# Fetching more tiles of embedding rows on SyncE and ScalarE, with a smaller descriptor store

## The chip, the core and the metric

The kernel runs on one core of a Trainium2 chip. The core has five engines that run side by side, each with a queue of instructions worked off in order: TensorE (PE; its weight loads are shown as PEld), VectorE (DVE), ScalarE (ACT), GpSimd (POOL) and SyncE (SP). Sixteen DMA engines move data between the chip's main memory and the core's on-chip memory; a transfer is issued by SP, ACT or POOL and tells of its landing by a semaphore. The metric is the device time of one execution in microseconds (us); lower is better.

## What is computed

A recommender's ranking network. For 16384 users there are 69 items each (`batch_user`) and one label item. Every item is a row of 96 floats in a table of 100001 rows. Each row is weighted by a small attention network against the label's row, the weighted rows are summed into 10 groups, and three layers follow.

```python
u  = emb[batch_user]                      # 16384 x 69 x 96
ql = emb[batch_label[:, 0]]               # 16384 x 96
q  = broadcast(ql)
z  = concatenate([q, u, q - u, q * u])    # 384 wide
h  = dice(z @ W1 + b1, a1)                # 64 wide
att = (h @ W2 + b2) @ W3 + b3
pre = where(batch_user < ITEM_NUM, u * att, 0)
pooled = einsum('gf,bfe->bge', window, pre)
x  = concatenate([pooled, ql])
h  = dice(bn(x @ Wf1 + bf1), af1)
h  = dice(bn(h @ Wf2 + bf2), af2)
out = h @ Wf3 + bf3
```

`dice` is a sigmoid gate, `bn` a constant scale. All is float32.

## The kernel before

The users are cut into 32 blocks of 512. A block's 512 x 69 rows are 69 chunks (64 of the main fields, 5 of the tail's), a chunk is four tiles of 128 rows, one row to a partition. Two chunks are a pair, and a pair is one step: there are 1104 steps (`NPAIR`). The order on every engine's queue is written out by hand: `plan` holds for each step the pieces of work in their order, and `at(step, ...)` appends to it.

What a step i does, in this order on each queue: every fourth step the attention rows of four pairs (`attend_rows`, PE matmul prow, ACT copy at L416) and a step later `spread` (PE patt, DVE rw); `hidden(i - 2)`: PE matmuls into ph (L399, L403), ACT's two activations (L405, L406), DVE's product y (L407); `scalar_rows(i)`: ACT's issues; `pool(i - 7)`: PE's acc matmuls on the pair's rows (L325), DVE's copy to pooled (L470); and `fetch(i)`: the rows of pair i are gathered, transposed by PE into two banks ptr (L325), and DVE makes uT (L376) and quT (L379) from each. Between these lie, once in a block, the label rows (`head_gather`, four gathers), and the top layers in ten pieces (`top_steps`, L502, L483, L484). The last eight steps have an order of their own (`CLOSE`).

The rows come in three ways:

- By POOL. `gather` (L266) issues one indirect DMA for a tile of 128 rows: 128 row numbers in, 128 x 96 floats out, into one of the eight places of a buffer u. `upool` has 14 such buffers; a pair's buffer is read by its transposes in step i and by `pool` seven steps later.
- By SP. A tile listed in `SP_CHUNKS` is fetched with 128 single DMAs of one row (384 bytes) each (L301) into a ring of `SP_RING` buffers. The row's address is in a register; `load` (L286) brings a group of addresses from the tile `offsets` into registers.
- By ACT, from `ACT_CHUNKS`, in the same manner, but a few rows in each step (`scalar_rows`), between its activations, into `ACT_RING` buffers.

In a listed chunk it is the fourth tile (`SLOT` = 3) that comes through the ring. PE waits for its semaphore (`wait_for_single`) and reads the ring's buffer in place of u. The first row of a tile into a buffer waits, through the framework, for the buffer's last readers, which are PE's acc matmuls. SP also loads the indices, `ids`, for four blocks at a time (L151), 50 steps ahead of the first of them, in the same queue.

Of the kernel before, what the change touches and what calls it, by code (L numbers as in the profile page):

```python
# [18 lines left out]
P = 128  # L19
# [29 lines left out]

ROW_BYTES = 4 * E  # L50
SLOT = 3
SP_CHUNKS = [2 * (10 * s + 8) + 1 for s in range(109)]
SP_RING = 4
ACT_CHUNKS = [2 * (8 * s + 11) for s in range(136)]
ACT_RING = 3
ACT_ROWS = 16
ACT_STEPS = -(-P // ACT_ROWS)
SINGLES = SP_CHUNKS + ACT_CHUNKS
NSB = (len(SINGLES) + P - 1) // P
NSEM = 8  # L60


def chunk_of(c):
# [52 lines left out]
def rec_kernel(  # L116
# [12 lines left out]
    nc = tc.nc  # L129
# [1 line left out]

    const = ctx.enter_context(tc.tile_pool(name="const", bufs=1))
    ipool = ctx.enter_context(tc.tile_pool(name="ipool", bufs=2))
    upool = ctx.enter_context(tc.tile_pool(name="upool", bufs=14))
    tpool = ctx.enter_context(tc.tile_pool(name="tpool", bufs=4))
    ypool = ctx.enter_context(tc.tile_pool(name="ypool", bufs=6))
    rpool = ctx.enter_context(tc.tile_pool(name="rpool", bufs=2))
# [137 lines left out]
    class Singles:  # L275

        def __init__(self, name, engine, kind, chunks, first, buffers, group):
            self.name, self.engine, self.kind, self.group = name, engine, kind, group
            self.chunks, self.first, self.buffers = chunks, first, buffers
            self.sems = [tc.alloc_semaphore(f"{name}{k}") for k in range(NSEM)]  # L280
            self.given = [0] * NSEM

# [12 lines left out]
        def fetch(self, s, start, stop):  # L295

            b, k = self.buffers[s % len(self.buffers)], s % NSEM
            for r in range(start, stop):
# [295 lines left out]
    def at(step, *work):  # L594
        plan.setdefault(step, []).extend(work)

    by_sync = Singles("sp", nc.sync, mybir.EngineType.SP, SP_CHUNKS, 0, range(SP_RING), 32)
    for s, m in enumerate(SP_CHUNKS):
        at(max(0, m // 2 - 6), lambda s=s: by_sync.fetch(s, 0, P))

    by_scalar = Singles(
        "act",
        nc.scalar,
        mybir.EngineType.Activation,
        ACT_CHUNKS,
        len(SP_CHUNKS),
        range(SP_RING, SP_RING + ACT_RING),
        2 * ACT_ROWS,
    )
    turn = {}  # L610
    for s, m in enumerate(ACT_CHUNKS):
        for k in range(ACT_STEPS):
            turn.setdefault(m // 2 - 2 - ACT_STEPS + k, []).append((s, k * ACT_ROWS, min(P, (k + 1) * ACT_ROWS)))

    def scalar_rows(i):

        for s, start, stop in turn.get(i, []):
            by_scalar.fetch(s, start, stop)

    c = NPAIR - CLOSE  # L620
    for i in range(c):
        if i >= 3 and (i - 3) % 4 == 3:
            at(i, rows_of(i - 6, 4))
        if i >= 3:
            at(i, tails_of(i - 3))
        if i >= 4 and (i - 4) % 4 == 3:
            at(i, spread_of(i - 7, 4))
        if i >= 2:
            at(i, hidden_of(i - 2))
        at(i, lambda i=i: scalar_rows(i))  # L630
        if i < c - CLOSE:
            if i >= POOL_LAG:
                at(i, pool_of(i - POOL_LAG))
        else:

            for k in {0: (-15, -14), 1: (-13,), 3: (-12, -11), 4: (-10, -9), 7: (-8, -7)}.get(i - c + 8, ()):
                at(i, pool_of(c + k))
        at(i, fetch_of(i))
# [116 lines left out]
```

## Time and profile before

| what | value |
|---|---|
| time, median of 3 executions | 10925.68 us (10925.35 to 10929.42) |
| profiled execution's own time | 10926.71 us |
| its span, from the first to the last instruction | 10924.9 us |
| granted TensorE clock, mean | 0.745 |
| POOL gathers | 8587 of u, 128 of q |
| rows issued by SP | 13952 |
| rows issued by ACT | 17408 |
| loads of row addresses | 436 on SP (median 2174 ns), 544 on ACT (median 2182 ns) |

The profile gives each engine's busy time; issues of DMAs, register moves and waits on the queues do not count as busy, so SP has no busy time at all and ACT's is without its row issues. Groups of instructions are named by line and by what they write and read: `u<-in_rows,ids` is a gather of rows. A line such as "2620.1 <-issue 2428.2" gives the idle time of the engine ahead of these instructions, and what ended most of it; "issue" means that nothing in the profile was waited for. In the timeline a name with a q (SPq, ACTq) stands for the engine's queue, and equal instructions are merged with their number behind an x.

### The profile page before, as it was taken

What the parts mean: (1) busy time and instruction counts of PE and PEld (TensorE: products, weight loads), DVE (VectorE), ACT (ScalarE), POOL (GpSimd) and SP (SyncE); (2) the same over time, 40 slices, a digit from 0 to 9 for tenths busy, and PEclk for the clock granted to TensorE, in tenths of its full rate; (3) what the DMA queues carried; (4) which work ended last, traced back from release to release, by engine and by line L of the source; (5) the groups of instructions that cost most, each with busy time, mean ns of one, the idle gap of its engine ahead of it and who ended that gap; (6) DMA issues with size and microseconds to landing.
All of it is one profiled execution on the core that took longest, in us unless ns stands there. A gap on an engine that the chain in (4) does not pass through costs nothing.

```text
span 10924.9 us, 172203 instructions
## 1 busy us (share of the span) xinstructions
PE 8862.0 (81%) x41797; PEld 4319.5 (40%) x41797; DVE 4285.5 (39%) x7535; ACT 1897.5 (17%) x2761; POOL 8226.3 (75%) x8721
## 2 busy tenths in 40 slices
PE   7878878788887888888878778878888887888878
PEld 3333434343333344333433333334343333433335
DVE  4334333333333333433333333333333333333334
ACT  1111111111111111111111111111111111111112
POOL 7777777777777777777777777777777777777776
PEclk7767777777777777767777777777777777777777
DMA  2212211121111212212111121112212112122111
GB/s 49 42 42 44 42 42 41 42 44 42 42 42 42 44 41 42 42 41 44 42 42 41 42 44 42 42 42 42 44 42 42 42 41 44 42 42 41 42 41 36
DMA packets 344467, 458.51 MB, mean 42 GB/s; under 512 B 202354, under 2 KB 202866, under 8 KB 343330
## 3 DMA queue, kind: packets, MB, share of 16 engines
q0 software_dynamic: 278880, 428.92, 18.7%
q1 hardware_dynamic: 29762, 11.82, 0.5%
q10 hardware_dynamic: 34816, 6.75, 0.4%
q8 instruction: 336, 5.51, 0.2%
q14 instruction: 673, 5.51, 0.2%
HBM read 446.74 MB, written 0.07 MB: 41 GB/s over the span
## 4 chain that ended last, share of the span: by engine, by line
POOL 49%; issue 21%; PE 17%; DMA 12%; DVE 0%; ACT 0%; ACTq 0%; POOLq 0%; DVEq 0%
POOL u L266 48%; DMA u<-in_rows,ids 12%; PE p L502 4%; PE acc L325 4%; PE ph L399 3%; PE ph L403 2%; PE ptr L325 2%; POOL q L266 1%; PE prow L414 1%; PE pa L423 1%; PE ph L396 0%; PE ph L401 0%; PE pc L348 0%; PE patt L431 0%; ACTq L301 0%
## 5 line engine op out<-in xcount | busy, mean ns | idle before, releaser
L266 POOL DMA_INDIRECT u<-in_rows,ids x8587 | 8104.3, 944 | 2620.1 <-issue 2428.2
L325 PE MATMUL ptr<-ident,u 128*96 128x128 f32 x8587 | 2002.8, 332 | 1940.1 <-DMA u<-in_rows,ids 1892.9
L407 DVE TENSOR_TENSOR y<-ph,y 128x512 f32<-128x512 f32 x1104 | 763.5, 692 | 4377.1 <-ACT y L406 4119.6
L325 PEld LDWEIGHTS ptr<-ident,u 128*96 128x96 f32 x8587 | 1139.7, 149 | 2701.4 <-DMA u<-in_rows,ids 2262.6
L325 PEld LDWEIGHTS acc<-rw,u 128*96 128x96 f32 x15930 | 1677.0, 187 | 1204.3 <-issue 977.6
L376 DVE COPY uT<-ptr 96x512 f32<-96x512 f32 x2208 | 1494.1, 677 | 1488.6 <-PE ptr L325 1485.2
L325 PE MATMUL acc<-rw,u 128*96 128x20 f32 x15930 | 1792.5, 258 | 57.8 <-DVE rw L436 41.7
L405 ACT ACTIVATE y<-ph 128x512 f32<-128x512 f32 x1104 | 658.6, 597 | 6308.6 <-PE ph L403 5822.7
L399 PE MATMUL ph<-uT,A 128*64 128x512 f32 x4096 | 1649.8, 883 | 0.0
L403 PE MATMUL ph<-quT,wn 96*64 96x512 f32 x4416 | 1585.2, 788 | 0.0
L379 DVE TENSOR_TENSOR quT<-ptr,qT 96x512 f32<-96x512 f32 x2048 | 1380.2, 674 | 0.0
L406 ACT ACTIVATE y<-y,wn,na1c 128x512 f32<-128x512 f32 x1104 | 898.1, 813 | 36.6
L403 PEld LDWEIGHTS ph<-quT,wn 96*64 96x64 f32 x4416 | 440.7, 188 | 1041.5 <-issue 1040.8
L502 PE MATMUL p<-pooled,wf 96*100 96x512 f32 (+1 forms) x1400 | 693.1, 644 | 0.0
L399 PEld LDWEIGHTS ph<-uT,A 128*64 128x64 f32 x4096 | 264.1, 175 | 616.2 <-issue 608.8
L416 ACT COPY row<-prow 128x512 f32<-128x512 f32 (+1 forms) x277 | 161.6, 583 | 1791.9 <-PE prow L414 1179.1
L470 DVE COPY pooled<-acc 96x160 f32<-96x160 f32 x1008 | 419.9, 417 | 117.6 <-PE acc L325 116.9
L414 PE MATMUL prow<-y,v 128*32 128x512 f32 x2208 | 453.6, 891 | 1.4 <-DVE y L407 1.1
L502 PE MATMUL p<-pre,V 96*100 96x512 f32 (+1 forms) x700 | 394.9, 710 | 3.0 <-DVE x L485 2.7
L502 PEld LDWEIGHTS p<-pooled,wf 96*100 96x100 f32 x1400 | 259.5, 198 | 332.6 <-issue 332.6
L436 DVE SCALAR_TENSOR_TENSOR rw<-patt,bb,wn 128x320 f32<-128x320 f32 x554 | 276.2, 539 | 143.6 <-PE patt L431 142.9
L431 PE MATMUL patt<-ident,row 128*128 128x128 f32 x1108 | 224.9, 340 | 25.1 <-DVE pre L424 22.7
(72 smaller groups left out, 2445.8 us busy)
## 6 DMA issues: line engine op xcount, KB each, us to landing
ring<-in_rows ACTq DMA_DIRECT2D x17408, 0.4 KB
ring<-in_rows SPq DMA_DIRECT2D x13952, 0.4 KB
u<-in_rows,ids POOLq DMA_INDIRECT x8587
ids<-in_idx SPq DMA_DIRECT2D x8, 560.0 KB, 3.9
q<-in_emb,ids POOLq DMA_INDIRECT x128
wf<-in_far SPq DMA_DIRECT2D x1, 1209.0 KB, 6.4
wn<-in_near SPq DMA_DIRECT2D x1, 236.0 KB, 2.8
ids<-in_idx SPq DMA_DIRECT2D x1, 140.0 KB, 2.3
```

The costliest lines, as they stand in the source:

```text
L266: nc.gpsimd.indirect_dma_start(out=dst, out_offset=None, in_=table, in_offset=bass.IndirectOffsetOnAxis(ap=index, axis=0),)
L325: ins = op(out, ring[:, at[0]].bitcast(F32) if at else u[:, 4 * (c % 2) + t, :], other, **how)
L376: nc.vector.tensor_copy(uT[j][0:E], ptr)
L379: nc.vector.tensor_tensor(quT[:, j, :].rearrange("e (s f) -> e s f", f=FM), ptr.rearrange("e (s f) -> e s f", f=FM), by_field(q[:, k * NS ...
L399: nc.tensor.matmul(p, As[n % 2][:, k // 4, :], uT[j], start=True, stop=False)
L403: nc.tensor.matmul(p, Wp, quT[:, j, :], start=False, stop=True)
L405: nc.scalar.activation(y, ph, AF.Sigmoid, scale=S_DICE)
L406: nc.scalar.activation(y, y, AF.Identity, bias=a1c, scale=na1c)
L407: nc.vector.tensor_mul(y, ph, y)
L414: nc.tensor.matmul(pr[32 * k : 32 * (k + 1), :], v2, ys[b + k], start=True, stop=True)
L470: nc.vector.tensor_copy(pooled[n][:, :, k * NS : (k + 2) * NS].rearrange("e g s -> e s g"), pa.rearrange("e j s g -> e (j s) g"),)
L502: nc.tensor.matmul(p1, w[:, h * DH : (h + 1) * DH], x, start=(k == 0), stop=(k == KTOP - 1))
```

## The change

- SP's list grows from 109 tiles, one in ten steps, to 199, one in five and a half. Its ring has 8 buffers for 4.
- ACT's list grows from 136 tiles to 170. Its rows are now one stream over all tiles, 20 in each step from step 0 on, where it was 16 in each of the eight steps of a tile. Addresses are still loaded 32 at a time; a step may now end one tile and begin the next. Its ring has 4 buffers for 3.
- A tile of ACT's is used two or three steps after the step that issues its last row; before it was three.
- `upool` has 15 buffers for 14.
- The kernel sets the size of the store that holds POOL's descriptors, in bytes of each partition, to 4096, where it left the framework's own.
- `offsets` grows to 384 columns for 256, as `NSB` follows the number of listed tiles.

```diff
-SP_CHUNKS = [2 * (10 * s + 8) + 1 for s in range(109)]
-SP_RING = 4
-ACT_CHUNKS = [2 * (8 * s + 11) for s in range(136)]
-ACT_RING = 3
-ACT_ROWS = 16
-ACT_STEPS = -(-P // ACT_ROWS)
+SP_CHUNKS = [2 * (int(5.5 * s) + 6) + 1 for s in range(199)]
+SP_RING = 8
+ACT_ROWS = 20
+ACT_CHUNKS = [2 * ((s + 1) * P // ACT_ROWS + 2) for s in range(170)]
+ACT_RING = 4
...
+RING_BYTES = 4096
...
-    upool = ctx.enter_context(tc.tile_pool(name="upool", bufs=14))
+    upool = ctx.enter_context(tc.tile_pool(name="upool", bufs=15))
...
-        2 * ACT_ROWS,
+        32,
     )
-    turn = {}
-    for s, m in enumerate(ACT_CHUNKS):
-        for k in range(ACT_STEPS):
-            turn.setdefault(m // 2 - 2 - ACT_STEPS + k, []).append((s, k * ACT_ROWS, min(P, (k + 1) * ACT_ROWS)))
-
     def scalar_rows(i):
 
-        for s, start, stop in turn.get(i, []):
-            by_scalar.fetch(s, start, stop)
+        row, stop = i * ACT_ROWS, min((i + 1) * ACT_ROWS, len(ACT_CHUNKS) * P)
+        while row < stop:
+            s, start = divmod(row, P)
+            n = min(P - start, stop - row)
+            by_scalar.fetch(s, start, start + n)
+            row += n
...
-    nc = bacc.Bacc("TRN2", target_bir_lowering=False, num_devices=1)
+    nc = bacc.Bacc("TRN2", target_bir_lowering=False, num_devices=1, dynamic_dma_scratch_size=RING_BYTES)
```

## The prediction

> **What bounds the kernel now.** I read the page's head, its groups and its chain first, then POOL's waits, then the chain at the end, and last the queues of SP and ACT, since the change loads these two.
>
> ```profile
> span 10924.9 us, 172203 instructions
> ...
> PE 8862.0 (81%) x41797; PEld 4319.5 (40%) x41797; DVE 4285.5 (39%) x7535; ACT 1897.5 (17%) x2761; POOL 8226.3 (75%) x8721
> ...
> POOL 49%; issue 21%; PE 17%; DMA 12%; DVE 0%; ACT 0%; ACTq 0%; POOLq 0%; DVEq 0%
> ...
> L266 POOL DMA_INDIRECT u<-in_rows,ids x8587 | 8104.3, 944 | 2620.1 <-issue 2428.2
> L325 PE MATMUL ptr<-ident,u 128*96 128x128 f32 x8587 | 2002.8, 332 | 1940.1 <-DMA u<-in_rows,ids 1892.9
> ```
>
> ```profile
> POOL u L266 <- issue: 2428.2, 7958, 0.3
> POOL u L266 <- DMA u<-in_rows,ids: 111.1, 364, 0.3
> ```
>
> POOL's 75% is a full engine: each gather is busy 0.944 us, then 0.30 us pass, and no idle stretch in its waits is longer than 0.3, whoever is named. The first of its 8715 gathers (8587 of u, 128 of q) starts at 3.30 us and the last at 10886.76: 1.2490 us apart on average, 1.2487 after the first hundred. PE waits 1893 us for their rows.
>
> ```profile
> 10748.20 2.47 DMA u<-in_rows,ids
> 10750.67 0.04 issue
> 10750.71 0.45 PE ptr L325
> 10751.16 5.12 PE p L502 x24
> ```
>
> This is the chain near the end. Up to 10748 us (about step 1085) it keeps coming back to a gather; from 10751 it is PE's closing work of some 174 us. So a gather removed before step 1085 takes its 1.2487 us off the end; a later one need not.
>
> **The gathers removed.** Single tiles go from 109+136 = 245 to 199+170 = 369, so POOL issues 124 gathers fewer: 8591. By step 1085 (m//2 counted over the lists) it is 366 against 243, thus 123: 123 x 1.2487 = 153.6 us. A step (one pair of chunks) shrinks from 8715 x 1.249 / 1104 = 9.86 us to 8591 x 1.249 / 1104 = 9.72 us. Every queue that now works more must fit into that.
>
> **SyncE: 25,472 rows instead of 13,952.** The trace has SP with its ring empty at the start, running without a wait:
>
> ```profile
> 6.33 243.65 SPq L301 DMA_DIRECT2D ring<-in_rows  x611
> ...
> SPq L301 <- PE ptr L325: 3556.9, 71, 95.2
> SPq L301 <- PE acc L325: 1324.8, 26, 96.8
> ```
>
> 243.65/611 = 0.399 us a row with the loads of row addresses (TENSOR_LOAD, median 2.17 us, four a tile) among them: 51.0 us a tile. By the tiles one by one, 48.7 us from first to last row and 2.6 to the next tile's first: 51.3 us. The change asks for a tile per 5.5 x 9.72 = 53.5 us, so SP is 96% full, and its 4882 us of waiting on PE nearly vanish. ScalarE's issues beside it do not slow it: rows follow each other at 0.3257 us while ACT issues, 0.3252 while it doesn't. 199 x 51.3 = 10,209 us against some 10,690 up to step 1095, where the last tile is used. With eight buffers a tile's buffer returns after 44 steps, of which it is held for 7 after its use, so the wait for PE at the head of each tile is over by then. Behind that wait in SP's queue stand the ids loads (L151, eight of them); they are placed 50 steps ahead of the block and needed 14 ahead, POOL's lead of 8 steps included 22: 28 steps of cover. The first one now stands behind tile 0, 55 us, and POOL wants it near step 12, 120 us. Cost: 0.
>
> **ScalarE: 21,760 rows, 20 a step for 16.** From two steps without idle time in its queue:
>
> ```profile
> 7013.77 0.60 ACT L405 ACTIVATE y<-ph 128x512 f32<-128x512 f32 x1 [1.31 <-PE ph L403]
> 7014.40 0.81 ACT L406 ACTIVATE y<-y,wn,na1c 128x512 f32<-128x512 f32 x1
> 7014.47 4.87 ACTq L301 DMA_DIRECT2D ring<-in_rows  x16
> 7019.38 0.60 ACT L405 ACTIVATE y<-ph 128x512 f32<-128x512 f32 x1 [4.17 <-PE ph L403]
> 7020.01 0.81 ACT L406 ACTIVATE y<-y,wn,na1c 128x512 f32<-128x512 f32 x1
> 7022.29 5.00 ACTq L301 DMA_DIRECT2D ring<-in_rows  x16
> ```
>
> L405 to the first row is 0.70 us; L406 runs beside the rows; an address load puts 2.21 us in (7022.29-7020.01 against 7014.47-7014.40). Sixteen rows take 4.8 to 5.55 us in this neighbourhood, so twenty 6.0 to 6.9, say 6.3. Loads are now one per 32 rows, 0.625 a step: 1.4. The copy of row (0.58 every fourth step), the top's g pairs and A's copies add 0.15 + 0.14 + 0.03. Sum 8.7 us, ends 8.4 and 9.3, of 9.72: 90% full, still under. What it delays: the next step's L405/L406 stand behind these rows, DVE's y L407 behind those, and behind it uT and quT of the newest pair, which free PE's two ptr banks. PE then starts a step later than it could; but PE has 9.72 - 8862/1104 = 1.7 us of slack a step, and POOL only feels PE after 15 u buffers less the 7 steps of lag: 8 steps, 78 us. In the trace the longest a gather's rows lay before PE took them was 25 us. Cover gone, it costs what ACT exceeds 9.72 by, per step. I take 0.
>
> At the closing PE is the chain. In steps 1073 to 1085 it catches up from 24 us behind POOL; POOL now makes four single tiles there for three, 1.2 to 2.5 us faster. I charge 1 us, ends 0 and 3. The 124 further ring tiles on PE add waits on semaphores: the present 245 ring transposes had no idle time before them. 0.
>
> **The smaller descriptor store and the fifteenth u buffer.** No gather waits for a buffer now, so the fifteenth brings nothing. The store is not seen as a thing in the trace. Lower bound 0: from the hundredth gather to the last the spacing never leaves 1.24 to 1.28 us. Upper bounds: the slow gathers at the start, in bunches such as
>
> ```profile
> 124.14 1.07 POOL L266 DMA_INDIRECT u<-in_rows,ids  x1 [0.30 <-issue]
> 125.51 1.07 POOL L266 DMA_INDIRECT u<-in_rows,ids  x1 [0.31 <-issue]
> 126.89 1.07 POOL L266 DMA_INDIRECT u<-in_rows,ids  x1 [0.30 <-issue]
> ```
>
> which make the first 98 average 1.275 us (128.26-3.30 over 98), 0.0264 more than the rest; and, further off, a gather that has to wait until an earlier one lands (2.47 us from start to landing, 1.5 more than the busy 0.94). Only two gathers are under way at once by that row (2.47/1.249), so I take 0 for any store that holds a handful.
>
> The Trainium skill, DMA: Bandwidth & Descriptors, states under Terms that a descriptor is 16 bytes and under The descriptor swizzle that a full transfer gives each engine nine, one of them the completion; a 4096-byte ring would by that hold 28 gathers, an estimate. No run here shows it.
>
> The same page, under Rules for kernel authors, speaks against the change: small transfers should be coalesced, since under 64 KB one pays mostly overhead, and under Anatomy of one DMA it puts a fixed 2.0 us on each. The rows above show 384-byte transfers leaving one queue every 0.33 us, so the fixed part overlaps. By the rule taken serially a tile would be 128 x 2.0 = 256 us and 199 of them 51 ms; by the row 10.2 ms.
>
> **The sum.** 10924.9 - 153.6 + 1 = 10772.3 us of span; the profiled run's time was 1.8 above its span and the median 1.0 below that run (10926.71 against 10925.68), so 10,773 us.
>
> **Rivals.**
> - *The store makes gathers dearer, and it ends slower than before.* Place: POOL's period. If the start's 0.0264 us stays for all 8591 gathers, +227 us: 11,000 us. It decides from 153/8591 = 0.018 us a gather, or one wait of 1.5 us per 85 gathers. For it: POOL has no idle time to hide anything. Against: after the first hundred nothing recurs, and the start also has the large loads beside it.
> - *SP becomes the bound.* It decides above 53.5 us a tile, 4% over what was measured. With rows at 0.35 us (tails of the spacing reach 0.355) a tile is 124 x 0.35 + 4 x 2.6 = 53.8, and 199 x 53.8 + 4, then some 90 us from step 1095 to the end: 10,800 us; at 54.1, 10,860. For it: never asked to run through before; against: the opening 611 rows did.
> - *The ACT-DVE-PE chain becomes the bound.* At ACT's upper 9.3 us with one L405 (0.60) waited for in every step, a step is 9.9 us; 1104 of them and the 40 us that the span has outside 1104 x 9.86 give 10,970 us; it decides from 9.72 and is slower than before from 9.86. For it: ACT, PE and SP at 90, 83 and 96%. Against: the 78 us of lead, and ACT's rows leave PE two steps.
> - *No change:* the shorter gather stream is given back by PE all through, 10,926. Against: 1893 us of PE's waiting are for gathers, ten times the gain.
>
> **How the numbers follow.** Forecast 0.73; SP 0.11; ACT chain 0.05, of which 0.01 ends faster, 0.02 within 0.2% and 0.02 slower; no change 0.01; the store 0.10, slower. The median can be told from no change at about 0.2%, 22 us. Faster 0.73 + 0.11 + 0.01 = 0.85, same 0.03, slower 0.12. The forecast by itself holds 10,764 to 10,790. Range 10,764 to 10,865: below, PE's closing 174 us 5% quicker (its granted clock there was 0.76); above, all of SP's rival.
>
> **What would show it.** Right: 8463 gathers of u at 944 ns, POOL's longest idle still 0.3, SP's waits on PE down to some 500 us, PE's wait for gathers down by about 150 us, ACT with less than 1.5 us of waiting a step, chain mostly POOL. Wrong: a gather period above 1.25 us (the store); PE ptr waiting on SP's ring rows, and POOL pausing on PE (SP); PE waiting on DVE uT or y with POOL pausing (ACT chain).

## The result and the profile after

The changed kernel takes 10,778.7 us (median of 4 executions, 10,777.35 to 10,782.2), the kernel before 10,925.51 us (10,925.12 to 10,929.42). The ratio is 0.9865, 95% interval [0.9853, 0.9877]: 147 us faster. The forecast was 10,773 us, 5.7 us less, with a range from 10,764 to 10,865.

The profiled execution took 10,782.2 us, the slowest of the four. From its page, the head, the chain's shares and the groups of the gathers and of the transposes that read them:

```profile
span 10780.4 us, 204439 instructions
...
PE 8756.9 (81%) x41797; PEld 4310.8 (40%) x41797; DVE 4235.1 (39%) x7535; ACT 1884.4 (17%) x2761; POOL 8110.8 (75%) x8597
...
POOL 40%; PE 21%; issue 19%; DMA 12%; ACTq 6%; ACT 2%; DVE 1%; POOLq 0%
...
L266 POOL DMA_INDIRECT u<-in_rows,ids x8463 | 7989.1, 944 | 2583.5 <-issue 2389.6
L325 PE MATMUL ptr<-ident,u 128*96 128x128 f32 x8463 | 1925.1, 332 | 1606.1 <-DMA u<-in_rows,ids 1555.6
```

POOL still has 75% busy time, now over a span that is 144.5 us shorter: 124 gathers fewer at the same 944 ns each. Of POOL's idle stretches none in the stream is longer than 0.3 us, as before:

```profile
POOL u L266 <- issue: 2389.6, 7828, 0.3
POOL u L266 <- DMA u<-in_rows,ids: 79.4, 260, 0.3
POOL u L266 <- PE ptr L325: 78.8, 258, 0.3
```

New in the chain is ACTq with 6%. SP's waits in the changed kernel:

```profile
SPq L530 <- DVE r L529: 416.6, 1, 416.6
SPq L301 <- PE ptr L325: 84.8, 36, 13.2
SPq L301 <- PE acc L325: 27.5, 7, 10.9
```

The first line is the store of the results at the end. Of the 4882 us that SP waited for PE inside its work, 112 are left. PE's longest waits; the second and third stood at 41.7 and 1.1 us before:

```profile
PE ptr L325 <- DMA u<-in_rows,ids: 1555.6, 1927, 2.2
PE acc L325 <- DVE rw L436: 177.6, 85, 7.2
PE prow L414 <- DVE y L407: 57.6, 25, 4.8
```

PE waits 337 us less for gathers, 136 us more for rw, which DVE can only make once ACT has copied row, and 57 us more for y, which stands behind ACT's activations. Last, two steps on ACT, in order of time (start, length, what; in brackets the engine's idle time before):

```profile
6004.07 0.60 ACT L405 ACTIVATE y<-ph 128x512 f32<-128x512 f32 x1 [7.26 <-PE ph L403]
6004.70 0.81 ACT L406 ACTIVATE y<-y,wn,na1c 128x512 f32<-128x512 f32 x1
6006.97 6.51 ACTq L301 DMA_DIRECT2D ring<-in_rows  x20
6013.59 0.60 ACT L405 ACTIVATE y<-ph 128x512 f32<-128x512 f32 x1 [8.07 <-PE ptr L325]
6014.22 0.81 ACT L406 ACTIVATE y<-y,wn,na1c 128x512 f32<-128x512 f32 x1
6014.28 8.72 ACTq L301 DMA_DIRECT2D ring<-in_rows  x20
6023.04 0.58 ACT L416 COPY row<-prow 128x512 f32<-128x512 f32 x1 [8.01 <-PE ph L403]
```

The rows fill the queue almost to the next activation: 6013.59 comes 0.11 us after the rows that began at 6006.97, and 6023.04 comes 0.04 us after the next ones. (The second stretch holds an address load among its rows.) Where the profile says that an activation waited for PE, its queue was still issuing.

### The profile page after: what moved, and what is told of

Same layout as the page of the kernel before. It is cut to its first block, busy times and chain, and to the rows that moved or that the text cites. A ratio compares the mean times of both kernels' runs of the same rounds, so it can differ in the third digit from the quotient of the medians.

```text
span 10780.4 us, 204439 instructions
## 1 busy us (share of the span) xinstructions
PE 8756.9 (81%) x41797; PEld 4310.8 (40%) x41797; DVE 4235.1 (39%) x7535; ACT 1884.4 (17%) x2761; POOL 8110.8 (75%) x8597
## 4 chain that ended last, share of the span: by engine, by line
POOL 40%; PE 21%; issue 19%; DMA 12%; ACTq 6%; ACT 2%; DVE 1%; POOLq 0%
POOL u L266 40%; DMA u<-in_rows,ids 12%; ACTq L301 4%; PE acc L325 4%; PE p L502 4%; PE ph L399 3%; PE ph L403 3%; PE ptr L325 2%; PE prow L414 1%; ACTq L286 1%; PE pa L423 1%; ACT y L405 1%; POOL q L266 1%; PE ph L396 1%; PE ph L401 1%
## 5 line engine op out<-in xcount | busy, mean ns | idle before, releaser
L266 POOL DMA_INDIRECT u<-in_rows,ids x8463 | 7989.1, 944 | 2583.5 <-issue 2389.6
L325 PE MATMUL ptr<-ident,u 128*96 128x128 f32 x8463 | 1925.1, 332 | 1606.1 <-DMA u<-in_rows,ids 1555.6
L399 PE MATMUL ph<-uT,A 128*64 128x512 f32 x4096 | 1598.9, 856 | 0.0
L403 PE MATMUL ph<-quT,wn 96*64 96x512 f32 x4416 | 1540.5, 767 | 0.0
L502 PE MATMUL p<-pooled,wf 96*100 96x512 f32 (+1 forms) x1400 | 667.7, 624 | 0.0
L414 PE MATMUL prow<-y,v 128*32 128x512 f32 x2208 | 507.2, 885 | 65.4 <-DVE y L407 57.6
L485 DVE SCALAR_TENSOR_TENSOR x<-p,wf,g 100x512 f32<-100x512 f32 (+3 forms) x105 | 73.9, 704 | 523.6 <-ACT g L484 523.5
```

The costliest lines, as they stand in the source:

```text
L266: nc.gpsimd.indirect_dma_start(out=dst, out_offset=None, in_=table, in_offset=bass.IndirectOffsetOnAxis(ap=index, axis=0),)
L325: ins = op(out, ring[:, at[0]].bitcast(F32) if at else u[:, 4 * (c % 2) + t, :], other, **how)
L399: nc.tensor.matmul(p, As[n % 2][:, k // 4, :], uT[j], start=True, stop=False)
L403: nc.tensor.matmul(p, Wp, quT[:, j, :], start=False, stop=True)
L414: nc.tensor.matmul(pr[32 * k : 32 * (k + 1), :], v2, ys[b + k], start=True, stop=True)
L502: nc.tensor.matmul(p1, w[:, h * DH : (h + 1) * DH], x, start=(k == 0), stop=(k == KTOP - 1))
```

## The experiments

Theory: the time is POOL's gathers times their spacing, plus a closing; SP and ACT cost nothing as long as each fits into a step; the 5.7 us that were missed come from ACT's rows in the closing. Rivals: the smaller store made gathers dearer; SP or ACT already sets the pace; the closing scatters by itself. Two numbers are read from each profile: where the last gather ends, and the closing, which is the time from there to the end. Before they are 10,887.7 and 37.2 us, in the changed kernel 10,735.6 and 44.9.

### The store alone

```diff
-    nc = bacc.Bacc("TRN2", target_bir_lowering=False, num_devices=1)
+    nc = bacc.Bacc("TRN2", target_bir_lowering=False, num_devices=1, dynamic_dma_scratch_size=4096)
```

> The kernel before with nothing changed but the descriptor store set to 4096. Gather-count theory: 8715 gathers as before, 10,925 to 10,928 us (each time the store is gone through costs some 8 ns by the traces of before and after, 306 times instead of 77, 2 us). Rival, that the store makes gathers dearer: if it explains the whole 6 us by which the changed kernel missed 10,773 us, 10,931 us or more, and if the opening's slow gathers stayed, 11,150 us.

Measured: 10,927.9 us (10 executions, 10,923.85 to 10,931.93) against 10,925.99 (16), ratio 1.0001 [0.9992, 1.0011]. Nothing that can be told apart. The trace tells more than the time: when the gathers are counted off in rounds of 28.44, the spacing at one place of the round is some 8 ns above the mean, everywhere else about 0.3 below; in the kernel before the same 8 ns come in rounds of 113.78, four times as long: a ripple. The round follows the size of the store, so it is read here as the number of gathers that fill it. The closing was 41.0 us here, with no queue's order changed: some 4 us of a closing's length can be scatter.

### Each half of the change alone

SyncE's part alone has ScalarE's list as before:

```diff
 SP_CHUNKS = [2 * (int(5.5 * s) + 6) + 1 for s in range(199)]
-ACT_ROWS = 20
-ACT_CHUNKS = [2 * ((s + 1) * P // ACT_ROWS + 2) for s in range(170)]
-ACT_RING = 4
+ACT_ROWS = 16
+ACT_CHUNKS = [2 * (8 * s + 11) for s in range(136)]
+ACT_RING = 3
...
+        for s, start, stop in turn.get(i, []):
+            by_scalar.fetch(s, start, stop)
```

> The changed kernel with ScalarE's list and order as before (136 tiles, 16 rows in each of a tile's eight steps, ring of 3); SyncE has its 199 tiles. Gather-count theory: 90 gathers fewer than before, 8625 at 1.249 us, last gather ends 112 us earlier, and the closing after it takes the 37 us of before since ScalarE has its old load: span 10,812, time 10,814 us. Rival, that PE's closing is longer for reasons that have nothing to do with ScalarE: the closing takes 44 us again, 10,821 us.

Measured: 10,818.97 us (10,815.74 to 10,821.25), ratio 0.9900 [0.9883, 0.9916]; last gather at 10,778.3, closing 41.2 us. The last gather ends 109 us earlier for 90 gathers, 1.22 us each. The closing is as long as in the run of the store alone, so the value between the two expectations does not tell them apart.

ScalarE's part alone has SyncE's list as before:

```diff
-SP_CHUNKS = [2 * (int(5.5 * s) + 6) + 1 for s in range(199)]
-SP_RING = 8
+SP_CHUNKS = [2 * (10 * s + 8) + 1 for s in range(109)]
+SP_RING = 4
```

> The changed kernel with SyncE's list and ring as before (109 tiles, ring of 4); ScalarE has its stream of 20 rows and 170 tiles. Gather-count theory: 34 gathers fewer than before, last gather 42 us earlier, and if ScalarE's rows are what stretches the closing, 44 us after it instead of 37: 10,890 us. Without that stretch: 10,883 us.

Measured: 10,892.1 us (7 executions, 10,885.67 to 10,896.72), ratio 0.9968 [0.9957, 0.9980]; last gather at 10,847.0, closing 39.8. Its scatter covers both expectations, but its closing is no longer than those of the two runs above, which have ScalarE's old load. The halves give 107.0 and 33.9 us, 140.9 together, the whole 146.8: the parts add up to within 6 us. The last gather's end moved by 1.22 and 1.20 us for each gather removed; by the times it is 1.19 and 1.00, and the seven executions of ScalarE's part lie 11 us apart.

### ScalarE's rows in the closing

The last three of ScalarE's tiles are left to POOL. It ran twice, the second time beside the changed kernel on one chip.

```diff
-ACT_CHUNKS = [2 * ((s + 1) * P // ACT_ROWS + 2) for s in range(170)]
+ACT_CHUNKS = [2 * ((s + 1) * P // ACT_ROWS + 2) for s in range(167)]
```

> The changed kernel with the last three of ScalarE's 170 tiles left to POOL, so that its rows end at step 1068 instead of 1087. Theory that ScalarE's rows delay PE in steps 1078 to 1087, where PE is behind POOL by 20 us anyway: three gathers more (3.7 us) are hidden behind PE, the closing after the last gather shrinks by more than that, 10,768 to 10,774 us. Rival, that POOL's count alone decides: 3.7 us slower than the changed kernel, 10,782 us.

> The changed kernel as it is, beside the next three on one chip: 10,775 to 10,782 us. Every theory expects the same; it is the measure for the others.

> e4 once more, in more rounds and beside the changed kernel. Theory that ScalarE's rows delay PE in the closing: 4 to 8 us below the changed kernel, whose closing its trace showed 10 us late at step 1088. Rival, that the closing's length only scatters: 4 us above it, for three gathers more.

Measured: 10,776.93 us (10,773.99 to 10,782.37) the first time; then 10,778.82 (10,777.28 to 10,782.46) beside the changed kernel's 10,781.01 (10,779.56 to 10,787.7). The chain that ended last, of the changed kernel between 10,520 and 10,612 us, its shares and three of its nine longest pieces (start, length, what):

```profile
by line: ACTq L301 38.1%; issue 11.9%; ACTq L286 11.5%; ACT y L405 5.8%; PE ph L396 4.1%; PE ph L403 4.0%; PE ph L401 3.7%; PE acc L325 3.0%; ACT y L406 2.9%; PE p L521 2.0%; PE p L502 1.9%; DVE y L407 1.5%; DVE uT L376 1.3%; DVE quT L379 1
...
10565.40 2.35 ACTq L286
10578.70 2.29 ACTq L286
10592.80 2.29 ACTq L286
```

and the same stretch of the second run without the three tiles:

```profile
by line: POOL u L266 51.8%; issue 21.4%; DMA u<-in_rows,ids 13.3%; PE p L502 6.0%; PE ph L399 2.2%; PE ph L403 1.9%; PE acc L325 1.4%; PE ptr L325 1.2%; PE prow L414 1.1%; POOLq L266 0.1%
...
10591.43 2.47 DMA u<-in_rows,ids
10600.17 2.47 DMA u<-in_rows,ids
10603.34 4.67 PE p L502 x24
```

In the changed kernel half of this stretch is ScalarE issuing rows and loading addresses; without them the chain goes back to gathers, so PE has caught up with POOL again. The closings after the last gather are 32.8 and 35.8 us against 44.9 and 47.7. In these profiled executions, then, ScalarE's last rows stretch the closing by some 12 us, 4 of which the three further gathers take back. They do so beside SyncE's longer list: with SyncE's old list the same rows left a closing of 39.8. But in the times of the other executions (three of each run, six against six) there is no such gain: 10,779.4 us on average against 10,779.4. By these times three gathers more, 3.7 us of POOL, show no cost, where the rival had them 3.7 us slower; the executions of either kernel lie 5 to 7 us apart, so a cost or a gain of 2 or 3 us could hide. The theory's 4 to 8 us of gain did not come either: beside each other the medians differ by 2.2. Why the profiled executions show more than the others was not tried.

### The store and the u buffers taken back

```diff
-    upool = ctx.enter_context(tc.tile_pool(name="upool", bufs=15))
+    upool = ctx.enter_context(tc.tile_pool(name="upool", bufs=13))
...
-    nc = bacc.Bacc("TRN2", target_bir_lowering=False, num_devices=1, dynamic_dma_scratch_size=RING_BYTES)
+    nc = bacc.Bacc("TRN2", target_bir_lowering=False, num_devices=1)
```

> The changed kernel with the store left at the framework's size, which leaves room for 13 u buffers in place of 15. Theory: neither part earns anything by itself; one ripple in 113.78 gathers instead of 28.44 saves 2 us, and POOL's lead of 6 steps, 58 us, still covers the 34 us that rows lie at most: 1 to 3 us below the changed kernel, within its scatter. Rival, that the fifteenth buffer is needed: idle stretches on POOL above 0.3 us and a longer time.

Measured: 10,780.44 us (10,778.72 to 10,783.11) beside the changed kernel's 10,781.01. POOL's longest idle stretch in the stream is 0.3 us as before, the closing is 45.0 us, and the spacing after the first hundred gathers is 1.2492 us, no shorter than with the small store. Neither the smaller store nor the fifteenth buffer earns anything; the gain is in the lists.

### How small a store may be

Both have the kernel before with another size in the first edit above, 512 and 256.

> The kernel before with the store at 512. By the ripple in the gathers' spacing (8 ns once in 28.44 gathers with 4096, once in 113.78 without the setting) a store of 4096 holds 28.44 gathers, so this one holds 3.6. Theory: a gather is under way for 2.5 us, two at once at a spacing of 1.249, so nothing waits; one ripple of 8 ns in 3.6 gathers, 2450 of them, 20 us: 10,945 us. Rival, that a store that is nearly full makes a gather wait: spacing above 1.3 us, 11,300 us or more.

> The kernel before with the store at 256, which holds 1.8 gathers by the same count, fewer than the two that are under way at once. Theory: now every gather waits until the one before it has freed its descriptors; spacing between 1.5 and 2.5 us, 13,000 to 21,800 us, with idle stretches on POOL above 0.3 us. Rival, that the size never matters: 10,960 us.

Measured: 11,178.9 us with 512 and 26,357.2 with 256, where the kernel before ran in 10,924.5. With 256 the time lies above theory and rival; with 512 it lies between them, 234 us above the theory and under the rival's 11,300. POOL's timeline with 512:

```profile
5017.21 0.95 POOL L266 DMA_INDIRECT u<-in_rows,ids  x1 [0.30 <-PE ptr L325]
5018.97 0.94 POOL L266 DMA_INDIRECT u<-in_rows,ids  x1 [0.80 <-issue]
5020.22 0.95 POOL L266 DMA_INDIRECT u<-in_rows,ids  x1 [0.31 <-issue]
```

and with 256:

```profile
5000.79 0.95 POOL L266 DMA_INDIRECT u<-in_rows,ids  x1 [2.12 <-issue]
5003.79 0.94 POOL L266 DMA_INDIRECT u<-in_rows,ids  x1 [2.04 <-issue]
5006.83 0.95 POOL L266 DMA_INDIRECT u<-in_rows,ids  x1 [2.10 <-issue]
```

A wait for store is idle time "from issue", before the gather, whose own length stays 0.94 us. With 256 every gather has it and the spacing is 3.02 us on average, 0.5 us more than a gather takes from start to landing. With 512 one gather in eleven starts later than 1.30 us after the one before, and the average spacing is 1.278. That is 0.029 us a gather and some 250 us in all, though by the count 3.6 gathers fit and two are under way.

### SyncE and ScalarE asked for more than they have

```diff
-SP_CHUNKS = [2 * (int(5.5 * s) + 6) + 1 for s in range(199)]
+SP_CHUNKS = [2 * (5 * s + 6) + 1 for s in range(218)]
```

> The changed kernel with SyncE's tiles one in 5 steps (218) instead of 5.5. A tile takes SyncE 51.45 us in the changed kernel's trace, 5 steps of POOL are 48.5. Theory: SyncE is the bound, 218 x 51.45 = 11,216 us to the last tile at step 1091 and some 125 us of closing: 11,345 us, PE waiting for the ring's rows and POOL pausing for u buffers. Rival, that POOL's count decides and SyncE only loses its lead: 19 gathers fewer, 10,756 us.

Measured: 11,368.0 us. PE's costliest wait in this run, and then POOL's two costliest that end with PE:

```profile
PE ptr L325 <- DMA ring<-in_rows: 1869.9, 192, 18.1
```

```profile
POOL u L266 <- PE ptr L325: 477.3, 230, 11.8
POOL u L266 <- PE acc L325: 170.8, 57, 14.7
```

PE waits for the ring 192 times, nearly once for each of the 218 tiles, and POOL, which had no idle stretch above 0.3 us, stops for up to 14.7 us for u buffers that PE has not freed. SP has no wait left inside its work; its tiles are 51.4 us apart and its last row goes out at 11,214 us, as expected; the rest is 152 us, 27 more than expected.

```diff
-ACT_ROWS = 20
-ACT_CHUNKS = [2 * ((s + 1) * P // ACT_ROWS + 2) for s in range(170)]
+ACT_ROWS = 24
+ACT_CHUNKS = [2 * ((s + 1) * P // ACT_ROWS + 2) for s in range(204)]
```

> The changed kernel with 24 rows a step on ScalarE (204 tiles). ScalarE waited 802 us in the changed kernel's trace, so its step of 20 rows takes 9.72 - 0.73 = 9.0 us; four rows more at 0.328 and an eighth of a load more at 2.4 make 10.6 us. Theory: ScalarE is the bound, 1088 x 10.6 and 160 us of closing: 11,690 us, with no waiting left on ScalarE. By the prediction's formula for its step (10.2 us) 11,260. Rival, POOL's count: 34 gathers fewer, 10,737 us.

Measured: 11,811.9 us, 1% above the expectation from the changed kernel's own steps and 5% above the prediction's formula. ACT's timeline of this run:

```profile
6009.09 0.60 ACT L405 ACTIVATE y<-ph 128x512 f32<-128x512 f32 x1 [9.14 <-issue]
6009.72 0.81 ACT L406 ACTIVATE y<-y,wn,na1c 128x512 f32<-128x512 f32 x1
6009.79 10.30 ACTq L301 DMA_DIRECT2D ring<-in_rows  x24
6020.13 0.59 ACT L416 COPY row<-prow 128x512 f32<-128x512 f32 x1 [9.59 <-PE acc L325]
6020.61 0.60 ACT L405 ACTIVATE y<-ph 128x512 f32<-128x512 f32 x1
```

A step is now rows, activation, rows, without a gap; everything else waits for it, POOL too. Both overloads take out more gathers than the changed kernel and are slower than the kernel before by 444 and 887 us.

### A version that is better than both

```diff
-SP_CHUNKS = [2 * (int(5.5 * s) + 6) + 1 for s in range(199)]
+SP_CHUNKS = [2 * (int(5.35 * s) + 6) + 1 for s in range(204)]
...
-ACT_CHUNKS = [2 * ((s + 1) * P // ACT_ROWS + 2) for s in range(170)]
+ACT_CHUNKS = [2 * ((s + 1) * P // ACT_ROWS + 2) for s in range(167)]
```

> The changed kernel with ScalarE's last three tiles left out and five more on SyncE (204, one in 5.35 steps, last used in step 1092). SyncE needs 204 x 51.45 = 10,496 us and 5.35 x 9.70 = 51.9 us a tile are there. Theory: two gathers fewer than the changed kernel and five fewer than e10, which count where PE has caught up: 6 us below e10, 10,765 to 10,770 us. Rival, that SyncE at 99% falls behind: PE waits for the ring and it is no faster than e10.

Measured: 10,772.36 us (10,771.52 to 10,775.94). All its executions lie below all of the changed kernel's beside it (10,779.56 and up), a median 8.6 us lower. Against the kernel before the ratio is 0.9861 [0.9844, 0.9877], beside 0.9867 [0.9851, 0.9884] for the changed kernel; these intervals do not separate the two, the single executions do. It is 6.5 us below the run without the three tiles, where 6 were expected, though 2 us above the range of times that was given. SP's waits in it:

```profile
SPq L301 <- PE ptr L325: 7.2, 28, 0.4
...
SPq L301 <- PE acc L325: 0.7, 3, 0.3
```

Some nine microseconds of waiting are all that SP has left inside its work, tiles follow each other every 51.4 us, and POOL still never pauses above 0.3 us: a queue can be filled to the last if what it feeds has some lead.

## Why the prediction was right

**POOL is the bound, and a gather removed takes its spacing off the end: shown.** 124 gathers fewer moved the last gather's end by 152.1 us where 154.8 were counted (124 x 1.2487); 90 and 34 fewer did so nearly in proportion. The 2.7 us short come from the spacing after the first hundred gathers, 1.2491 us where the prediction kept 1.2487. The store's ripple would by its count make 1.9 us of this (8.3 ns, 302 rounds for 77), and with the store alone the spacing was 1.2489. But with the store taken back it was 1.2492, and in the changed kernel's second profile 1.2494: profiles of one kernel differ by nearly as much as the rise, so its cause stays open.

**SyncE fits: shown, and how far.** A tile took 51.5 us (51.3 forecast) against 53.5. At 48.5 us a tile it became the bound as that rival had it, and the time of its last row follows from tiles times 51.4. The Trainium skill's rule to coalesce small transfers (DMA: Bandwidth & Descriptors, Rules for kernel authors) did not bear here: 25,472 of 384 bytes left SP at 0.40 us each, address loads included, and the last gather came earlier by nearly all that was taken from POOL. (The fixed 2.0 us that the prediction took from that page's Anatomy of one DMA stands there for DMAs of GpSimd's path, not for SyncE's.) The sign "SP's waits on PE down to some 500 us" was misjudged: 112 are left. The 417 at the final store, a wait for DVE, are of another kind and were 451 before.

**ScalarE fits: shown, with less room than forecast.** Its step took some 9.0 us rather than 8.7: up to its last row, in 1088 steps of 9.75 us, its queue waited some 0.8 us a step for work. A load and the way to its first row took 2.40 us where 2.21 had been read off one step, and rows followed each other at 0.328 us with the slow first rows counted in, where 0.315 was taken. The upper end, 9.3, held it.

**POOL's lead covers what PE loses: shown.** PE took rows up to 33.5 us after their gather's end (at 10,652 us, near the closing), longest before 24.9; the cover was put at 78. With 13 buffers, hence 58, nothing changed.

**The closing was sized too small.** The prediction charged 1 us, ends 0 and 3, for PE's closing; it grew from 37.2 to 44.9 us in the profiles. On the profiled span of 10,780.4 us, 8.1 above the sum's 10,772.3, this miss is 6.6 us and the gathers' is 1.5 (152.1 for 153.6): nothing cancelled. Four microseconds of that can be scatter, by the run of the store alone. What speaks for ScalarE's rows beside the closing's work, which the prediction had considered for the middle of the kernel but not for steps 1078 to 1087, where PE catches up: with them and SyncE's new list the profiles show 44.9, 47.7 and 45.0 us, without the last three tiles 32.8, 35.8 and 37.4. Against it as a cause by itself: 39.8 with SyncE's old list. In the other executions the effect is not seen beyond the 3.7 us that the last three tiles fail to earn, so its size stays open.

**The rival of the dear store had the right place and point, not the right size at 4096.** Its breaking point was 0.018 us a gather. The opening's 0.026 did not last (0.0004 and 0.0007 instead, in the changed kernel's two profiles). At 512 the cost is 0.029 us in the kernel before; by that figure a change with that store would have lost its gain, which was not run. By the Trainium skill a descriptor has 16 bytes and a transfer of 1 MiB to 128 partitions gives each DMA engine nine to write (DMA: Bandwidth & Descriptors, Terms and The descriptor swizzle). Taken over for a gather of 128 rows, that makes 28.4 gathers in 4096 bytes, an estimate, and the ripple at 28.44 agrees.

**Waiting that moved.** The prediction expected PE's wait for gathers to fall by about 150 us. It fell by 337: PE's other waits, above all for rw and y, rose by 298 us in all and its busy time fell by 105, which with the 144.5 us of span makes up the number. None of this reached POOL.

## What to carry to other kernels

When one engine issues without a gap, the gain of taking work from it is the number of instructions times their spacing, provided that each queue that takes the work over still fits into the shortened step: read its rate from a stretch of the trace where it waited for nothing, and hold it against the demand. On SyncE 96% and 99% of such a rate were free here, 106% cost more than the whole gain. A store for descriptors may be cut while it holds many times what is under way; near the number under way it costs at once.

## What was not expected of the hardware

- POOL's store shows itself in the spacing of gathers as a ripple of 8 ns, once in 28.44 gathers with 4096 and once in 113.78 without the setting. Read as the store's capacity in gathers, it can be had from a trace without any experiment; the waits at 512 and 256 fit that reading.
- A store for 3.6 gathers already makes gathers wait (2.3% of the time) although two are under way at a time, and one for 1.8 gathers spaces them by 3.02 us, longer than the 2.5 us from start to landing. This fits a place in the store that comes free later than its gather's rows land; the store itself is not seen in a trace.
- With gathers 3.02 us apart, the mean granted TensorE clock was 0.58, against 0.745 before; PE was busy 11,016 us for the same matmuls, where it had been 8,862. Its busy share had fallen from 81% to 42%. But with SyncE too fast the share fell to 71% and the clock was 0.765, with 8,020 us busy: idle time alone does not set it, and what does was not tried.
